# Two-layer graph and expert kernel: additions of kept outputs behind an eviction, five small loads on another queue, one part's statistics behind the first factors

## The chip, the cores and the metric

The kernel runs on one core of one Trainium2 chip. The metric is the device time of one execution in microseconds (us), lower is better. Three timed runs of the kernel before gave 2253.24, 2259.94 and 2261.37 us; the median is 2259.94. The profiled execution is another one, and its own time is in the section on the profile.

The core has TensorE (PE, with its weight loads PEld), VectorE (DVE), ScalarE (ACT), GpSimd (POOL) and SyncE (SP). Each has its own queue of instructions, which it works off in the order in which they stand there. In this kernel SP does nothing but issue DMAs; POOL and ACT issue some too.

## The reference

8192 nodes of 256 features (128 graphs of 64 nodes) pass two layers. Each layer adds a graph part and an expert part to x:

```python
# layer 0
x = x + softplus(xn @ W_self + (I - s_out*adj*s_in) @ xn @ W_neigh)   # xn: layer norm twice, gamma, beta
H = gelu(LN(x) @ W1 + b1); probs = softmax(H @ Wg + bg); e = argmax(probs)
x = x + probs[e] * (H @ Wd[e] + bd[e])                                # 8 experts, one per node
# layer 1
x = x + gelu(LN(attention(LN(x), adj)) * gamma + beta)                # attention within a graph
scores = LN(edge_softmax_sum(LN(x) @ W_gat, edge_index)).mean(heads)  # 1048576 random edges
w, top = softmax(top_k(scores, 2))                                    # 2 of 4 experts
for e in range(4):
    x = x + gate[e] * (gelu(LN(x0) @ W1[e] + b1[e]) @ W2[e] + b2[e])  # x0: x before the experts
```

All of it is float32, the matrices too.

## The kernel before

**Layout.** x stays in on-chip memory as `x[P, NT, D]`: 64 tiles of 128 nodes with 256 features. Four tiles make a group g (16 groups), two groups make a part (8 parts). The code is written as Python generators. A generator traces instructions and yields at points where another may take a turn; small loops decide whose turn it is. The trace order is then only a priority: a scheduler that has times of its own for every instruction places each on its engine's queue, and may place one ahead of others that were traced before it, if it thinks that its inputs will be there. `with tc.issue_after(ins):` adds an edge from `ins` to each instruction traced in the block on the engine of `ins`: they stand behind it on that queue. It adds no semaphore.

**The start (L418 to L577).** SP loads adjacency, x and weights in turn (L510, L142, L514). GpSimd's queue holds the making of constants, the clearing of block buffers (L522), and five small loads: b1 (L421), wg (L425), bg (L428), gcol (L526) and bcol (L528). b1, gcol and bcol are read so that feature p of a block goes to partition p: one float per element. wg is read as eight floats per element. For a part, `look` takes the statistics of its eight tiles (`bn_stats`, L548), has GpSimd copy the adjacency into block form (L553), lets TensorE sum columns into one PSUM buffer (L557), and VectorE copies the sums out (`deg`, L560). `make` works these into scale factors by about twenty small VectorE operations (L561 to L577, with L153 to L166): `fac` and `shift`. The first graph unit (`graph`, L586) has ScalarE scale x by them, and TensorE transpose the result; gcol and bcol are used as the transpose is copied out (L606). wg, b1 and bg are first used by the gated units, after about 80 us. The trace order of the start is: `look(0, -1)`, `make(-1)`, `look(1, 0)`, and then, in the mixing loop, graph units beside `make(0)` and further parts.

**The middle.** Up to 540 us graph and gating units run beside the collecting of edge keys; then the layer-0 experts of nodes sorted by expert (L928), layer 1's attention, and the edges of the second graph part. Units of the layer-1 experts (`experts`, L1068 matmuls ph, L1078 matmuls py, L1082 evictions) run beside these. In all that time the gates are not known, so outputs y are stored in DRAM (`ystore`, L1104): 28 tiles, 24 with four experts' outputs and four with three.

**The stage of pairs (about 1855 to 2164 us).** 32 of the 64 tiles are routed: their nodes are sent to slots by chosen expert, in pairs of 128-row tiles, 38 pairs in two halves. For a pair m, `pairs` loads the rows `zin` (L1990) and the expert's weights `w1e` (L1992) two pairs ahead with three buffers each, computes the hidden part in four steps (matmuls ph, L2021; gelu on ScalarE, L2025), transposes the next pair's rows (L2004), computes two output groups (matmuls py, L2034, two PSUM buffers), which VectorE evicts as `y` (L2042) and SP stores in `yslots` (L2043). It yields seven times a pair. At every third yield a step of sending or fetching rows by indirect DMA gets its turn (L1868, L2054, with the additions of L2065), and at every ninth yield a step of `kept`.

**`kept` (L1941 to L1955).** At its call n it loads the kept outputs of the nth of these 28 tiles into `yin` (L1950, two buffers, 512 or 384 KB), and adds those of tile n-1, three or four experts, each with a call of `add` (L1934): x += gate * y, 128x256. After the fourth addition of a tile its x is complete and SP stores it (L1937). The load is held behind `behind[0]`, the last w1e load or output store traced, so that it isn't issued too early on SP. The additions have no such edge. After the pairs come the units left over (from 2164 us), whose additions are made straight from y.

Of the kernel before, what the change touches and what calls it, by code (L numbers as in the profile page):

```python
# [15 lines left out]
ALU = mybir.AluOpType  # L16
# [4 lines left out]
P = 128  # L21
NT = 64
N = P * NT
D = 256
GR = 4
# [55 lines left out]
def kernel(  # L81
# [31 lines left out]
    nc = tc.nc  # L113
    V, S = nc.vector, nc.scalar
    FD = f0_w1.shape[1]
    NH = FD // P
    E0 = f0_wg.shape[1]
# [21 lines left out]
    x = const.tile([P, NT, D], F32, name="x")  # L139
# [20 lines left out]
    def moments(raw, sm, df, var):  # L160

        V.tensor_tensor(sm, raw[:, :, :, 1], raw[:, :, :, 4], ALU.add)
        V.tensor_tensor(df, raw[:, :, :, 1], raw[:, :, :, 4], ALU.subtract)
        V.tensor_tensor(var, raw[:, :, :, 2], raw[:, :, :, 5], ALU.add)
        V.scalar_tensor_tensor(df, df, 0.25, df, ALU.mult, ALU.mult)
        V.scalar_tensor_tensor(var, var, 1.0 / D, df, ALU.mult, ALU.add)  # L166
# [251 lines left out]
    with tc.tile_pool(name="w0", bufs=1, reuse_waits="tile") as w0, tc.tile_pool(name="kp", bufs=1, reuse_waits="tile") as kp:  # L418
        w1 = w0.tile([P, 2, FD], F32, name="w1")
        b1 = w0.tile([P, NH], F32, name="b1")  # L420
        nc.gpsimd.dma_start(b1, f0_b1.rearrange("(q p) -> p q", p=P))  # L421

        wg = w0.tile([P, NH, 32], F32, name="wg")
        nc.gpsimd.memset(wg, 0.0)
        nc.gpsimd.dma_start(wg[:, :, 0:E0], f0_wg.rearrange("(q p) e -> p q e", p=P))  # L425
        bg = w0.tile([P, 1], F32, name="bg")
        nc.gpsimd.memset(bg, 0.0)
        nc.gpsimd.dma_start(bg[0:E0, :], f0_bg.rearrange("(e o) -> e o", o=1))  # L428

        sel = w0.tile([P, E0], F32, name="sel")  # L430
        V.tensor_reduce(sel, ident.rearrange("p (j e) -> p e j", j=4)[:, 0:E0, :], AX.X, ALU.add)
# [16 lines left out]
        with tc.tile_pool(name="b2", bufs=2, reuse_waits="tile") as b2, tc.tile_pool(name="bh", bufs=NH + 2, reuse_waits="tile") as bh, tc.tile_pool(  # L448
# [25 lines left out]
            with tc.tile_pool(name="bg1", bufs=1, reuse_waits="tile") as bg1, tc.tile_pool(name="bg2", bufs=2, reuse_waits="tile") as bg2, tc.tile_pool(  # L474
# [48 lines left out]
                V.tensor_tensor(wcat[:, :, 0:D], wcat[:, :, 0:D], wcat[:, :, D : 2 * D], ALU.add)  # L523
                V.tensor_scalar(wcat[:, :, D : 2 * D], wcat[:, :, D : 2 * D], -1.0, None, ALU.mult)
                gcol = bg1.tile([P, 2], F32, name="gcol")
                nc.gpsimd.dma_start(gcol, g0_gamma.rearrange("(c p) -> p c", p=P))  # L526
                bcol = bg1.tile([P, 2], F32, name="bcol")
                nc.gpsimd.dma_start(bcol, g0_beta.rearrange("(c p) -> p c", p=P))  # L528

# [1 line left out]
                M = PART * GR  # L533
# [9 lines left out]
                def look(part, i):  # L543

                    raw, deg = found[i]
                    dps = psg0.tile([P, GR * P], F32, name="ms")
                    for k in range(M):
                        V.bn_stats(raw[:, 1, k, :], x[:, part * M + k, :])  # L548
                    for j in range(PART):
                        b = raws[j]  # L550
                        tsl = slice(part * M + j * GR, part * M + j * GR + GR)
                        for h in HALVES:
                            nc.gpsimd.tensor_copy(b[h, :, h], adj[h, tsl, :])  # L553
                        yield
                        for k in range(GR):
                            at = j * GR + k
                            nc.tensor.matmul(dps[:, at : at + 1], b[:, k, :], ones_col, start=True, stop=True)  # L557
                        V.tensor_reduce(deg[:, 1, j * GR : j * GR + GR], adj[:, tsl, :], AX.X, ALU.add)
                        V.tensor_scalar(on[:, tsl, :], adj[:, tsl, :], 0.0, None, ALU.is_gt)
                    V.tensor_copy(deg[:, 0, :], dps[:, 0:M])  # L560
                    yield  # L561

                def make(i):
                    raw, deg = found.pop(i)
                    sm, df, var = (bg2.tile([P, 2, M], F32, name=n) for n in ("sm", "df", "var"))
                    ve, guess, work = (bg2.tile([P, 4, M], F32, name=n) for n in ("ve", "guess", "work"))
                    moments(raw, sm, df, var)
                    V.tensor_scalar(ve[:, 0, :], var[:, 0, :], EPS, None, ALU.add)


                    V.tensor_scalar(ve[:, 1, :], var[:, 1, :], EPS, EPS, ALU.add, ALU.mult)
                    V.tensor_tensor(ve[:, 1, :], ve[:, 1, :], var[:, 1, :], ALU.add)
                    V.scalar_tensor_tensor(ve[:, 2:4, :], deg, 0.0, deg, ALU.is_equal, ALU.add)
                    to = fac[:, i + 1]
                    root_of_bits(to, ve, guess, work)
                    V.scalar_tensor_tensor(shift[:, i + 1], sm, -0.5, to[:, 0:2, :], ALU.mult, ALU.mult)
                    V.scalar_tensor_tensor(to[:, 2:4, :], deg, 0.0, to[:, 2:4, :], ALU.not_equal, ALU.mult)  # L577

                def graph(g):

# [180 lines left out]
                for _ in look(0, -1):  # L761
                    pass
                make(-1)
                next_found(0)
                for _ in look(1, 0):
                    pass
# [92 lines left out]
                last = V.tensor_copy(slot_t, es).ins  # L859

            with tc.tile_pool(name="bs", bufs=3, reuse_waits="tile") as bs, tc.tile_pool(
# [80 lines left out]
                for g in range(beside):  # L942
# [6 lines left out]
                    last = unit  # L949
# [49 lines left out]
    b1 = wp.tile([P, NEXP, NH1], F32, name="b1")  # L999
# [54 lines left out]
    to = {}  # L1054
    adds = []
    n_kept = [0] * DENSE
    pace = []
    behind = []

    def experts(g, take):  # L1060

        zT = zTs.pop(g)
        for e in range(NEXP):
            hTs = []
            for q in range(NH1):
                ph = to["ph"]()
                for c in range(2):
                    nc.tensor.matmul(  # L1068
                        ph, w1[:, e, c, q * P : q * P + P], zT[:, c, :], start=(c == 0), stop=(c == 1)
                    )  # L1070
                hT = to["hT"]()
                pace[:] = [S, S.activation(hT, ph, AF.Gelu, bias=b1[:, e, q : q + 1]).ins]  # L1072
                hTs.append(hT)
                yield "h"
            for k in range(GR):
                py = to["py"]()
                for q in range(NH1):
                    nc.tensor.matmul(  # L1078
                        py, hTs[q][:, k * P : k * P + P], w2[:, e, q, :], start=(q == 0), stop=(q == NH1 - 1)
                    )  # L1080
                y = to["y"]()
                pace[:] = [V, V.tensor_tensor(y, py, b2[:, e * D : e * D + D], ALU.add).ins]  # L1082
                take(e, k, y)
                yield "y"

# [847 lines left out]
    def add(t, e, y):  # L1933
        V.scalar_tensor_tensor(x[:, t, :], y, gate[:, e, t : t + 1], x[:, t, :], ALU.mult, ALU.add)  # L1934
        added[t] = added.get(t, 0) + 1
        if added[t] == NEXP:
            behind[:] = [nc.sync.dma_start(out_t[:, t, :], x[:, t, :]).ins]  # L1937
# [3 lines left out]
    def kept():  # L1941

        ys = {}
        ts = [t for t in range(T0) if n_kept[t // GR]]
        for n in range(len(ts) + 1):
            if n < len(ts):
                g, k = divmod(ts[n], GR)
                ys[n] = f2.tile([P, NEXP * D], F32, name="yin")[:, 0 : n_kept[g] * D]
                with tc.issue_after(behind[0]):
                    nc.sync.dma_start(ys[n], ystore[g, k, :, 0 : n_kept[g] * D])  # L1950
            if n:
                t, y = ts[n - 1], ys.pop(n - 1)
                for e in range(n_kept[t // GR]):
                    add(t, e, y[:, e * D : e * D + D])
            yield  # L1955

    with tc.tile_pool(name="gd", bufs=1, reuse_waits="tile") as gd:
# [14 lines left out]
    def pairs():  # L1972
# [39 lines left out]
        for m, (h, i) in enumerate(of):  # L2012
            e, _, w1e, b1e, b2e = loaded.pop(0)
            zT = ahead
            if m + 2 < len(of):
                loaded.append(load(*of[m + 2]))
            hTs = []
            for q in range(NH1):
                ph = to["ph"]()[:, 0 : 2 * P]
                for c in range(2):  # L2020
                    nc.tensor.matmul(  # L2021
                        ph, w1e[:, c, q * P : q * P + P], zT[:, c, :], start=(c == 0), stop=(c == 1)
                    )
                hT = to["hT"]()[:, 0 : 2 * P]
                pace[:] = [S, S.activation(hT, ph, AF.Gelu, bias=b1e[:, q : q + 1]).ins]  # L2025
                hTs.append(hT)
                yield h
            if m + 1 < len(of):
                ahead = turned(loaded[0][1])
            yield h  # L2030
            for k in range(2):
                py = to["py"]()
                for q in range(NH1):
                    nc.tensor.matmul(  # L2034
                        py,
                        hTs[q][:, k * P : k * P + P],
                        w2[:, e, q, :].rearrange("p e f -> p (e f)"),
                        start=(q == 0),
                        stop=(q == NH1 - 1),
                    )  # L2040
                y = to["y"]()
                pace[:] = [V, V.tensor_tensor(y, py, b2e, ALU.add).ins]  # L2042
                nc.sync.dma_start(yslots[h][(2 * i + k) * P : (2 * i + k + 1) * P, :], y)  # L2043
                yield h

# [99 lines left out]
```

## Time and profile before

| what | value |
|---|---|
| profiled execution, its own time | 2238.6 us |
| its span, first to last instruction | 2236.6 us |
| median of the timed runs | 2259.94 us |
| TensorE clock granted, mean | 0.966 |
| PE busy | 2072.5 us (93%) |
| DVE busy | 1526.6 us (68%) |
| ACT busy | 920.8 us (41%) |
| POOL busy | 446.6 us (20%) |

The busy time of the engines by stretch:

| stretch, us | PE busy | DVE busy | ACT busy | DMA share |
|---|---|---|---|---|
| 0 to 56 | 39.90 | 37.84 | 26.43 | 0.81 |
| 56 to 168 | 101.40 | 98.68 | 84.20 | 0.16 |
| 1855 to 1965 | 105.92 | 31.46 | 40.61 | 0.86 |
| 1965 to 2005 | 35.28 | 10.66 | 11.90 | 0.74 |
| 2060 to 2165 | 93.91 | 36.96 | 32.64 | 0.67 |
| 2165 to 2236 | 67.65 | 34.34 | 18.42 | 0.36 |

A row of the page's groups names a line, an engine, an operation and what it writes and reads, then the count, the busy time, the mean duration in ns, and how long the engine had been idle ahead of it and for whom. "SPq" is the issuing of DMAs on SyncE. A tile carved out of `wd`'s space, as most of the first stage's are, is called `wd` in the profile. A matrix product in float32 shows as two records for each matmul of the code. The difference between the profiled execution and the timed runs (21 us) is between executions of the same program.

### The profile page before, as it was taken

Reading aid. Unit: us, or ns where it says so; the run is one execution under the profiler, and the core shown is the slowest. Engines: PE = TensorE matmul, PEld = TensorE weight load, DVE = VectorE, ACT = ScalarE, POOL = GpSimd, SP = SyncE. Lnnn points to the kernel's source line nnn. Section 1 sums busy time; section 2 is a strip of 40 time slices with the busy share of each in tenths; the row PEclk is TensorE's granted clock in tenths of the full one; section 3 lists DMA queues with packets and bytes.
Section 4 is the critical chain, followed back from the end, with each engine's and each line's share of the span. In section 5 each row is a group of like instructions: output and inputs, shape, how many; then the busy total and the mean of one; then the engine's idle time right before and its main releaser. Section 6 shows DMA issues by size and latency. Waiting matters only on the chain. (4 is left out here: it accounts for less than half of the span.)

```text
span 2236.6 us, 31405 instructions
## 1 busy us (share of the span) xinstructions
PE 2072.5 (93%) x10046; PEld 1391.4 (62%) x10046; DVE 1526.6 (68%) x4539; ACT 920.8 (41%) x1662; POOL 446.6 (20%) x469
## 2 busy tenths in 40 slices
PE   7899999897999999999867889998999999999999
PEld 4444444443667667666545666765777767878776
DVE  6898997924899999994188766666788552323335
ACT  4776766664211211222157556432333333323322
POOL 3011111112000000000062100004666552303213
PEclk9999999998999999999987989999999999999999
DMA  8021122232111112112123211282222148878843
GB/s 226 25 75 50 50 65 69 79 99 76 38 55 57 38 53 57 34 53 71 46 83 119 88 40 41 77 247 58 60 58 61 43 149 251 280 223 251 257 131 98
DMA packets 206731, 219.82 MB, mean 98 GB/s; under 512 B 53200, under 2 KB 174416, under 8 KB 206560
## 3 DMA queue, kind: packets, MB, share of 16 engines
q1 hardware_dynamic: 181296, 182.37, 26.6%
q0 software_dynamic: 17056, 35.09, 5.8%
q8 instruction: 85, 1.39, 0.3%
q10 hardware_dynamic: 8208, 0.26, 0.2%
q14 instruction: 86, 0.70, 0.1%
HBM read 132.66 MB, written 84.91 MB: 97 GB/s over the span
## 5 line engine op out<-in xcount | busy, mean ns | idle before, releaser
L466 PE MATMUL ph<-zT,w 128*128 128x512 f32 x1056 | 506.6, 611 | 10.4 <-ACT zT L694 6.0
L469 ACT ACTIVATE hT<-ph,b 128x512 f32<-128x512 f32 x264 | 180.4, 686 | 492.8 <-PE ph L466 492.5
L466 PEld LDWEIGHTS ph<-zT,w 128*128 128x128 f32 x1056 | 190.5, 193 | 194.5 <-issue 169.8
L928 PE MATMUL py<-wd,hT 128*128 x1088 | 250.6, 382 | 0.0
L296 DVE TENSOR_TENSOR one<-iota_l,pb 128x1024 bf16<-128x1024 bf16 x192 | 233.2, 1215 | 1.5 <-PE cnt_ps L307 1.5
L928 PEld LDWEIGHTS py<-wd,hT 128*128 128x128 f32 x1088 | 201.0, 190 | 24.8 <-issue 0.5
L1550 POOL DMA_INDIRECT got<-tsrc,esrc x144 | 165.8, 1152 | 201.4 <-DMA zslots<-none 86.8
L1146 POOL DMA_INDIRECT yin<-yrows,row_y x64 | 64.7, 1011 | 667.3 <-SPq L991 562.5
L1078 PE MATMUL py<-w,hT 128*128 128x256 f32 x800 | 191.0, 389 | 7.3 <-DVE kt L1483 4.7
L1068 PE MATMUL ph<-zT,w 128*128 128x512 f32 x400 | 184.9, 604 | 0.0
L1078 PEld LDWEIGHTS py<-w,hT 128*128 128x128 f32 x800 | 150.3, 193 | 37.4 <-issue 13.4
L2034 PE MATMUL py<-w,hT 128*128 x608 | 142.1, 388 | 16.8 <-DVE y L2042 16.8
L1934 DVE SCALAR_TENSOR_TENSOR x<-yin,gate,x 128x256 f32<-128x256 f32 x108 | 52.1, 484 | 151.5 <-DMA yin<-ystore 149.1
L1072 ACT ACTIVATE hT<-ph,b 128x512 f32<-128x512 f32 x100 | 68.6, 687 | 210.1 <-PE ph L1068 208.5
L2025 ACT ACTIVATE hT<-ph,b1e 128x256 f32<-128x256 f32 x152 | 71.8, 473 | 199.9 <-PE ph L2021 118.6
L2021 PE MATMUL ph<-zTp,w1e 128*128 128x256 f32 x608 | 139.9, 384 | 4.1 <-DMA w1e<-in_L_ffn_W_dram 4.1
L2034 PEld LDWEIGHTS py<-w,hT 128*128 128x128 f32 x608 | 114.7, 194 | 34.2 <-DVE y L2042 19.4
L296 DVE TENSOR_TENSOR one<-iota_h,pb 128x512 bf16<-128x512 bf16 x192 | 130.7, 683 | 0.0
L2021 PEld LDWEIGHTS ph<-zTp,w1e 128*128 128x128 f32 x608 | 117.1, 193 | 20.6 <-issue 4.3
L620 PE MATMUL pre<-wd 128*128 128x512 f32 x256 | 127.8, 613 | 1.5 <-ACT wd L606 1.3
L750 POOL DMA_INDIRECT zrows<-z,pos x64 | 63.7, 995 | 281.8 <-issue 94.9
L1068 PEld LDWEIGHTS ph<-zT,w 128*128 128x128 f32 x400 | 73.6, 191 | 72.0 <-issue 71.0
(414 smaller groups left out, 3447.1 us busy)
## 6 DMA issues: line engine op xcount, KB each, us to landing
w1e<-in_L_ffn_W_dram SPq DMA_DIRECT2D x38, 512.0 KB
yin<-ystore SPq DMA_DIRECT2D x24, 512.0 KB
ystore<-y SPq DMA_DIRECT2D x80, 128.0 KB
zslots<-none SPq DMA_DIRECT2D x38, 256.0 KB
zin<-zslots SPq DMA_DIRECT2D x38, 256.0 KB
yslots<-y SPq DMA_DIRECT2D x76, 128.0 KB
zin<-zrows SPq DMA_DIRECT2D x68, 128.0 KB
bd<-in_L_ffn_bd_dram SPq DMA_DIRECT2D x68, 128.0 KB
```

Source lines behind the costliest of these rows:

```text
L296: V.tensor_tensor(o, wi.unsqueeze(1).to_broadcast([P, HK, n]), pb[:, g : g + HK].unsqueeze(2).to_broadcast([P, HK, n]), ALU.is_equal,)
L466: nc.tensor.matmul(ph, w1[:, c, q * P : q * P + P], zT[:, c, :], start=(c == 0), stop=(c == 1))
L469: gelus.append(S.activation(hT, ph, AF.Gelu, bias=b1[:, q : q + 1]).ins)
L620: nc.tensor.matmul(pre, xnT[:, c, n * P : n * P + P], wcat[:, c, :], start=(c == 0), stop=(c == 1),)
L928: nc.tensor.matmul(py, hTs[q][:, k * P : k * P + P], wd[:, bass.ds(ex[k], 1), q, :].rearrange("p e f -> p (e f)"), start=(q == 0), stop=(q ...
L1068: nc.tensor.matmul(ph, w1[:, e, c, q * P : q * P + P], zT[:, c, :], start=(c == 0), stop=(c == 1))
L1072: pace[:] = [S, S.activation(hT, ph, AF.Gelu, bias=b1[:, e, q : q + 1]).ins]
L1078: nc.tensor.matmul(py, hTs[q][:, k * P : k * P + P], w2[:, e, q, :], start=(q == 0), stop=(q == NH1 - 1))
L1550: nc.gpsimd.indirect_dma_start(got, None, tsrc, bass.IndirectOffsetOnAxis(ap=esrc[:, b, at : at + 1], axis=0))
L2021: nc.tensor.matmul(ph, w1e[:, c, q * P : q * P + P], zT[:, c, :], start=(c == 0), stop=(c == 1))
L2025: pace[:] = [S, S.activation(hT, ph, AF.Gelu, bias=b1e[:, q : q + 1]).ins]
L2034: nc.tensor.matmul(py, hTs[q][:, k * P : k * P + P], w2[:, e, q, :].rearrange("p e f -> p (e f)"), start=(q == 0), stop=(q == NH1 - 1),)
```

## The change

It does three things. `experts` and `pairs` keep the last eviction traced in `sums`, and `kept` traces its additions behind it on VectorE's queue. The five small loads at the start are issued from ScalarE's queue and not GpSimd's. `make` keeps the last instruction of each set of factors, and the second part's statistics (`look(1, 0)`) are put behind the last one of the first set; the later parts' are traced as before.

```diff
-        nc.gpsimd.dma_start(b1, f0_b1.rearrange("(q p) -> p q", p=P))
+        nc.scalar.dma_start(b1, f0_b1.rearrange("(q p) -> p q", p=P))
...
-        nc.gpsimd.dma_start(wg[:, :, 0:E0], f0_wg.rearrange("(q p) e -> p q e", p=P))
+        nc.scalar.dma_start(wg[:, :, 0:E0], f0_wg.rearrange("(q p) e -> p q e", p=P))
...
-        nc.gpsimd.dma_start(bg[0:E0, :], f0_bg.rearrange("(e o) -> e o", o=1))
+        nc.scalar.dma_start(bg[0:E0, :], f0_bg.rearrange("(e o) -> e o", o=1))
...
-                nc.gpsimd.dma_start(gcol, g0_gamma.rearrange("(c p) -> p c", p=P))
+                nc.scalar.dma_start(gcol, g0_gamma.rearrange("(c p) -> p c", p=P))
...
-                nc.gpsimd.dma_start(bcol, g0_beta.rearrange("(c p) -> p c", p=P))
+                nc.scalar.dma_start(bcol, g0_beta.rearrange("(c p) -> p c", p=P))
...
-                    for k in range(M):
-                        V.bn_stats(raw[:, 1, k, :], x[:, part * M + k, :])
+                    with tc.issue_after(first_made[0]) if part == 1 else ExitStack():
+                        for k in range(M):
+                            V.bn_stats(raw[:, 1, k, :], x[:, part * M + k, :])
...
-                    V.scalar_tensor_tensor(to[:, 2:4, :], deg, 0.0, to[:, 2:4, :], ALU.not_equal, ALU.mult)
+                    last = V.scalar_tensor_tensor(to[:, 2:4, :], deg, 0.0, to[:, 2:4, :], ALU.not_equal, ALU.mult)
+                    first_made.append(last.ins)
+
+                first_made = []
...
                 pace[:] = [V, V.tensor_tensor(y, py, b2[:, e * D : e * D + D], ALU.add).ins]
+                sums[:] = pace[1:]
...
-                for e in range(n_kept[t // GR]):
-                    add(t, e, y[:, e * D : e * D + D])
+                with tc.issue_after(sums[0]):
+                    for e in range(n_kept[t // GR]):
+                        add(t, e, y[:, e * D : e * D + D])
...
                 pace[:] = [V, V.tensor_tensor(y, py, b2e, ALU.add).ins]
+                sums[:] = pace[1:]
```

More of the change, by code (lines that the diff above doesn't have):

```diff
@@ L1057 @@
     pace = []
+    sums = []
     behind = []
```

## The prediction, made before the changed kernel was run

> **What bounds the kernel now.** I read four views, in this order: the chain of waits on the page, the waits of the stage 1850 to 2165 us, that stage's busy time in windows with the timelines of three engines around one stall, and the timelines of the first 35 us. The chain reaches back only to 1519 us, where a loop guard joins all engines; before that the busy table must do, and there TensorE is busy 93% of the span.
>
> ```profile
> PE 26%; DMA 3%; DVE 1%; issue 1%; SPq 1%; POOL 0%; ACT 0%; DVEq 0%; ACTq 0%; POOLq 0%
> PE py L1078 7%; PE ph L1068 6%; PE py L2034 5%; PE ph L2021 4%; DMA yin<-ystore 2%; PE pd L1562 1%; PE ps L1594 1%; PE ph L2004 0%; DMA w1e<-in_L_ffn_W_dram 0%; PE ps L1500 0%; DVE x L1934 0%; DVE y L2042 0%; DMA yslots<-y 0%; DVE x L2065 0%; DMA zslots<-y,place 0%
> ```
>
> The reader is to see that the end is set by matmuls, and that the one large entry beside them is a load: yin<-ystore, the kept expert outputs that `kept` fetches (L1950). 2% of 2236.6 us is 45 us of chain. Not all of it is lost: matmuls run during part of it. The waits of the stage say who passes it on:
>
> ```profile
> DVE x L1934 <- DMA yin<-ystore: 149.1, 25, 10.3
> ...
> DVE y L2042 <- PE py L2034: 49.3, 24, 12.3
> ...
> PEld py L2034 <- DVE y L2042: 19.4, 11, 4.4
> PE py L2034 <- DVE y L2042: 16.8, 8, 4.2
> ```
>
> Columns: us waited in total, times, longest. VectorE waits 149 us in 25 waits at L1934, the additions; that alone costs nothing. But TensorE then waits for VectorE's evictions (L2042), because the additions stand ahead of these on VectorE's queue. One stall in full (VectorE, SyncE and TensorE lines of their timelines):
>
> ```profile
> 1991.15 0.75 DVE L2042 TENSOR_TENSOR y<-py,b2e 128x256 f32<-128x256 f32 x2
> 2002.25 1.01 DVE L1934 SCALAR_TENSOR_TENSOR x<-yin,gate,x 128x256 f32<-128x256 f32 x2 [10.35 <-DMA yin<-ystore]
> 2003.17 0.42 DVE L2042 TENSOR_TENSOR y<-py,b2e 128x256 f32<-128x256 f32 x1
> ...
> 1995.47 0.42 SPq L1950 DMA_DIRECT2D yin<-ystore  x1
> ...
> 2003.64 5.41 PE L2034 MATMUL py<-w,hT 128*128 x16 [4.12 <-DVE y L2042]
> ```
>
> The load is issued at 1995.47 and lands at 2002.2; the eviction behind it follows at 2003.17, and TensorE, with both py buffers full, starts 4.12 us late. Its group takes 5.41 us where undisturbed ones take 3.46 (the second half waits again): 1.95 us more, 6.1 us in all.
>
> How much is lost in all? By the chain, py groups of successive pairs start at 1866.17 and, thirteen pairs on, at 1961.89: 7.36 us a pair. From 1961.89 to the stage's end at 2163.79 are 201.9 us; 24 pairs at 7.36 and one last py group of 3.46 are 180.1. So **21.8 us** are lost, all after 1962 (the first thirteen pairs hide VectorE's waits of up to 8.4 us).
>
> At the start:
>
> ```profile
> 7.42 0.78 POOL L526 DMA_DIRECT2D gcol<-in_L_gnn_gamma_dram  x1
> 9.14 1.75 POOL L553 COPY wd<-wd 64x256 f32<-64x256 f32 x4
> ...
> 10.82 1.73 DVE L548 BATCH_NORM_STATS2 raw<-x 128x6 f32<-128x256 f32 x5 [1.02 <-DMA x<-in_x_dram]
> 13.00 0.69 DVE L523 TENSOR_TENSOR wd<-wd 128x512 f32<-128x512 f32 x1 [0.45 <-DMA wd<-in_L_gnn_W_neigh_dram]
> 16.29 0.75 DVE L548 BATCH_NORM_STATS2 raw<-x 128x6 f32<-128x256 f32 x2
> 20.84 0.17 DVE L560 COPY deg<-ms 128x8 f32<-128x8 f32 x1 [1.21 <-PE ms L557]
> 23.04 0.16 DVE L576 SCALAR_TENSOR_TENSOR shift<-sm,fac 128x16 f32<-128x16 f32 x1
> ...
> 23.24 2.57 ACT L586 ACTIVATE wd<-x,shift,fac 128x256 f32<-128x256 f32 x5 [11.09 <-DVE shift L576]
> ```
>
> ScalarE begins the first graph unit at 23.24 us, on factors finished at 23.1. The first part's statistics and moments are through at 16.29; then the second part's eight statistics are threaded into the chain of small factor operations, and at 20.84 it also waits for the second part's degree copy.
>
> **What the skill says.** (1) The Trainium skill, "DMA: Bandwidth & Descriptors", section "Anatomy of one DMA", says that DMA engines don't wait on semaphores: the wait is on the issuing sequencer. The trace agrees: SyncE issued one pair's w1e at 1961.64 straight after an output store at 1961.05, whose additions ended at 1961.0. A late addition thus holds other loads too. (2) The same page, "Rules for kernel authors", says that a strided last dimension becomes one descriptor per element; no view read here counts descriptors for the small loads, but a like load on SyncE (b1, L1009, 2048 single floats) occupied its issue for 2.47 us. (3) The same page, "Issuing engines are not separate DMA queues": moving a load to another issuer saves that issuer's time only. The trace's DMA share of 0.83 to 1.15 in the first 40 us shows the engines they all share to be full then.
>
> **The change part by part.**
>
> *Additions behind an eviction.* `kept` is called at every ninth yield of `pairs`, which yields seven times a pair. Tile t's additions are therefore traced at yield 9t+17, behind 2 x floor((9t+17)/7) evictions, plus 1 or 2 where the remainder is 5 or 6. The new edge makes that the earliest place. Counting L2042 ahead of each L1934 group on VectorE gives today's place: tile 10 has 28 evictions ahead and gets at least 30; tile 13, 34 and 38; tile 16, 44 and 46; tile 19, 51 and 54; tile 23, 62 and 64; tile 24, 64 and 66; tile 25, 67 and 68. Over tiles 0 to 26 the gain is 0 to 4 evictions, mostly 2 to 4, each 7.36 / 2 = 3.7 us of matmul. The longest wait is 10.35 us, at tile 13, which gains 14.7 us; tile 10's 9.71 us meets 7.4 us, but only the part past its own eviction's readiness was lost (0.6 us there). No instruction is added. Behind the waiting addition stand the next evictions and output stores; the load of tile t+2 takes tile t's buffer (two buffers), so it must not be pushed late. By trace order, load t+2 follows w1e of two pairs ahead, which is free when the previous pair's hidden matmuls end. The latest case has its additions behind the second eviction of two pairs before that; they need 0.4 + 4 x 0.5 = 2.4 us of the 3.45 us of those hidden matmuls, so they finish about 1 us ahead. From load issue to the additions at least py, hidden and py again lie: 10.8 us against 6.7 us measured above. Tile 25 gains one eviction only and tile 18 none; I leave 3 us of the 21.8. Bounds: 22 gained if no load is late, 8 if half the waits come back through SyncE's queue. I take **19**.
>
> *Second part's statistics behind the first factors.* Eight at 0.34 us apart (1.73 us for five) leave the chain: 2.7 us. The 1.21 us wait can go as well: with no fillers the chain may end before the second part's degree copy, which stays free to move. So 2.7 to 3.9, upper value taken. They run right after; their user is the second factors, whose scaling starts at 32.09 on ScalarE, 9 us later, so that is the cover.
>
> *Small loads to ScalarE's queue.* GpSimd loses 1.09 + 0.93 + 0.56 + 0.78 + 0.74 = 4.1 us of issuing; its copies (9.14) can start near 5.6, where the adjacency has landed. That is hidden: the statistics wait for x until 10.82. ScalarE gains five issues; at 0.5 to 2.5 us each (SyncE's usual issue and the L1009 one) that is 2.5 to 12.5 us from about 1 us on, and it does nothing else until 23.24. By one element per descriptor they make 1024 + 1024 + 8 + 512 = 2568 packets. On ScalarE's queue now, 8208 packets take 0.2% of 16 engines' span, 8.7 ns each; 2568 x 8.7 / 16 = 1.4 us that x and W_neigh may land later. An estimate: bounds 0 and 4 us, should issues of SyncE queue up behind them; I take 1.4. gcol and bcol are needed at 26.3 today, near 22 then.
>
> Start: 3.9 - 1.4 = **2.5 us**, bounds -2 and 5. From there TensorE is busy 90% or more, so a head start is kept; other work is threaded anew in the first 540 us, which can give or take 3 us.
>
> Sum: 19 + 2.5 = 21.5. Against the profiled execution (2238.6 us, span 2236.6) that is 2217; the timed runs lie 21 us above it, and the loss is of the same nature there, so I take it off their median: 2259.94 - 21.5 = **2238**.
>
> **Rivals.**
> - *The transfer takes the place of the queue.* Evictions flow, but yin, w1e and outputs are issued late on SyncE and pairs wait for weights. For it: the DMA share of 0.86 in 1855 to 1965, and one SyncE queue for all. Against: those thirteen pairs ran at full rate at that share. Gain 8 at the least, 0 at the start: 2252.
> - *Slower: the load's buffer.* If additions end up later than traced by over about 1 us past the hidden matmuls, SyncE stops at each yin load with the next w1e behind it. w1e is issued two pairs ahead, 14.7 us, of which landing takes 6 to 7 and SyncE's lag about 3; below 5 us of stop it is free, beyond that each of 26 loads pays the excess. At 6.5 us of stop: 26 x 1.5 = 39 lost on top of a gain of 19: 2280. For it: two buffers only, 1 us of margin. Against: the scheduler places additions where their eviction is due, and a full pair more is needed.
> - *The start goes the other way.* Small packets delay x and W_neigh by 4 us, factors come 2 us later or are rethreaded badly: 2260 - 19 + 5 = 2246.
> - *The edge moves nothing* would be 2260; the counts above exclude it for tiles 10 to 25.
>
> **How the numbers follow.** Forecast 0.62, start the other way 0.14, transfer 0.14 (with the last rival), slower 0.10. What this measurement can tell from no change is 0.5%, 11.3 us: faster 0.76, same 0.14, slower 0.10. Forecast alone: gains of 12 to 27, 2233 to 2248. The timed runs scatter from 2253 to 2261, and the transfer rival at 2252 is taken in: 2226 to 2254.
>
> **What would show it.** Right: L1934's waits for yin fall from 149 us to a few, TensorE's waits for L2042 vanish, py groups keep 7.36 us through 2164; L576 near 19 to 21 us, and L586 follows it. Wrong: TensorE waiting for w1e or zin; yin issued later against its pair than today; the first L548 after 12 us; a first graph unit held by gcol or bcol at L606.

## The result, and the profile after

| | before | after |
|---|---|---|
| median of 5 timed runs, us | 2259.94 (2251.79 to 2262.57) | 2237.92 (2232.50 to 2241.17) |
| profiled execution, us | 2238.6 | 2232.5 |
| its span, us | 2236.6 | 2230.4 |

The ratio is 0.9909, 95% interval 0.9881 to 0.9936: 22 us less, between 14 and 27. The two profiled spans differ by 6.2 us only, so the profiles have to be read stretch by stretch before the 22 us are found in them. I take marks that both have: the first `shift`, the last scatter of the layer-0 gating, the last store of the layer-0 experts, the first gather of the edges, the first and the last py matmul of the pairs. "Attention" is from the last expert store to the first gather, "edges" from there to the first py.

```
                     first   gating  experts  edges   first   last    atten-
                     shift   end     end      begin   py      py      tion    edges   pairs   span
before                23.0   549.0   1109.0   1506.3  1866.0  2163.4  397.3   359.7   297.4   2236.6
after                 21.6   545.4   1105.4   1509.3  1882.6  2157.2  403.9   373.3   274.6   2230.4
```

The pairs lost 22.8 us. 3.6 us came up to the end of the gating, and 20.2 us were given back in attention and edges, in which nothing was changed: from the first attention step to the first pairs, every engine has the same instructions in the same order in both kernels. Those 20.2 us are what the first and the last experiment are about.

The pairs first. The chain of waits of the changed kernel, as the page has it:

```profile
PE 29%; DVE 2%; issue 1%; DMA 0%; another core or an unknown queue 0%; SPq 0%; DVEq 0%
PE py L1084 6%; PE ph L1074 6%; PE ph L2030 6%; PE py L2043 6%; PE ps L1601 2%; PE pd L1569 2%; PE ph L2013 1%; DVE rows L1500 0%; PE ps L1507 0%; DMA w1e<-in_L_ffn_W_dram 0%; DVE y L1088 0%; DVE ol L1457 0%; PE ps L1531 0%; DVE to L1563 0%
```

Lines have moved: the additions are now L1941, the pairs' matmuls ph and py L2030 and L2043, their evictions L2051, the load of yin L1957. The load of the kept outputs, 2% before, is gone from the chain, and the shares of both kinds of pair matmuls are larger. The waits from 1840 to 2160 us (us in total, times, longest):

```profile
DVE y L2051 <- PE py L2043: 139.5, 60, 12.2
...
DVE x L1941 <- DMA yin<-ystore: 5.9, 5, 2.6
...
PE ph L2030 <- DMA w1e<-in_L_ffn_W_dram: 3.9, 1, 3.9
```

VectorE's 149 us of waiting for yin have become 5.9, and it waits for TensorE in their place, 139.5 us, as one expects where TensorE is the bound. In this view TensorE doesn't wait for an eviction any more; its one wait is for the first pair's weights. VectorE's timeline at one such place:

```profile
1987.40 0.42 DVE L2051 TENSOR_TENSOR y<-py,b2e 128x256 f32<-128x256 f32 x1 [3.24 <-PE py L2043]
1989.13 0.42 DVE L2051 TENSOR_TENSOR y<-py,b2e 128x256 f32<-128x256 f32 x1 [1.30 <-PE py L2043]
1989.78 2.05 DVE L1941 SCALAR_TENSOR_TENSOR x<-yin,gate,x 128x256 f32<-128x256 f32 x4 [0.23 <-DMA yin<-ystore]
1994.75 0.42 DVE L2051 TENSOR_TENSOR y<-py,b2e 128x256 f32<-128x256 f32 x1 [2.92 <-DMA out_dram<-x]
```

Two evictions, then four additions, then about 3 us of nothing until the next pair's outputs are due. (The view puts the last wait down to a store; the py group whose first half that eviction takes had begun at 1992.98.) Before, the additions stood ahead of two evictions and held them. The stage's timeline on the chain gives a pair every 7.35 us without a break, from 1882.79, where the first pair's py group starts, to 2157.6.

The start, with VectorE's lines and then GpSimd's, TensorE's and ScalarE's from their own timelines:

```profile
10.04 1.74 DVE L550 BATCH_NORM_STATS2 raw<-x 128x6 f32<-128x256 f32 x5 [1.26 <-DMA x<-in_x_dram]
13.75 0.15 DVE L562 COPY deg<-ms 128x8 f32<-128x8 f32 x1
17.62 0.17 DVE L562 COPY deg<-ms 128x8 f32<-128x8 f32 x1 [3.21 <-PE ms L559]
21.60 0.17 DVE L578 SCALAR_TENSOR_TENSOR shift<-sm,fac 128x16 f32<-128x16 f32 x1
21.78 2.70 DVE L550 BATCH_NORM_STATS2 raw<-x 128x6 f32<-128x256 f32 x8
24.42 0.40 DVE L600 TENSOR_TENSOR wd<-wd,fac 64x256 f32<-64x256 f32 x1
33.54 0.17 DVE L578 SCALAR_TENSOR_TENSOR shift<-sm,fac 128x16 f32<-128x16 f32 x1
...
6.51 1.89 POOL L555 COPY wd<-wd 64x256 f32<-64x256 f32 x4 [2.02 <-DMA wd<-in_adj_dram]
...
25.40 1.09 PE L617 MATMUL tz<-ident,wd 128*128 128x128 f32 x4 [0.77 <-DVE wd L600]
...
1.35 0.89 ACTq L425 DMA_DIRECT2D wg<-in_L_ffn_Wg_dram  x1
2.27 1.46 ACTq L526 DMA_DIRECT2D gcol<-in_L_gnn_gamma_dram  x1
```

Before, the scaling and the second factors stood here:

```profile
23.65 0.40 DVE L595 TENSOR_TENSOR wd<-wd,fac 64x256 f32<-64x256 f32 x1
29.80 0.17 DVE L576 SCALAR_TENSOR_TENSOR shift<-sm,fac 128x16 f32<-128x16 f32 x1
```

GpSimd's copies do start sooner (6.51 for 9.14), and x isn't later for the small loads (10.04 for 10.82). The statistics of the second part are out of the chain: they run in one piece after the factors. But the second part's degree copy has stayed in it and costs 3.21 us in place of 1.21. The first factors come 1.4 us sooner (over all profiles with the same start 21.2 to 21.6 us, where three of the start before have 22.3 to 23.0). What follows them is not all sooner: the first unit's adjacency scaling (L600), at 23.65 before, is now behind the eight statistics at 24.42, and TensorE waits 0.77 us for it; and the second factors come at 33.54, where they came at 29.80.

### The profile page after: what moved, and what is told of

Same layout as the page of the kernel before. It is cut to its first block, busy times and chain, and to the rows that moved or that the text cites. A ratio compares the mean times of both kernels' runs of the same rounds, so it can differ in the third digit from the quotient of the medians.

```text
span 2230.4 us, 31413 instructions
## 1 busy us (share of the span) xinstructions
PE 2067.0 (93%) x10046; PEld 1387.5 (62%) x10046; DVE 1526.1 (68%) x4539; ACT 922.5 (41%) x1663; POOL 441.3 (20%) x464
## 5 line engine op out<-in xcount | busy, mean ns | idle before, releaser
L2030 PE MATMUL ph<-zTp,w1e 128*128 128x256 f32 x608 | 140.0, 384 | 3.9 <-DMA w1e<-in_L_ffn_W_dram 3.9
L2051 DVE TENSOR_TENSOR y<-py,b2e 128x256 f32<-128x256 f32 x76 | 32.2, 424 | 157.3 <-PE py L2043 139.5
L2043 PE MATMUL py<-w,hT 128*128 x608 | 137.5, 379 | 0.0
L2030 PEld LDWEIGHTS ph<-zTp,w1e 128*128 128x128 f32 x608 | 117.2, 193 | 20.5 <-issue 4.1
L2043 PEld LDWEIGHTS py<-w,hT 128*128 128x128 f32 x608 | 112.6, 190 | 13.8
```

The source lines that it names most:

```text
L2030: nc.tensor.matmul(ph, w1e[:, c, q * P : q * P + P], zT[:, c, :], start=(c == 0), stop=(c == 1))
L2043: nc.tensor.matmul(py, hTs[q][:, k * P : k * P + P], w2[:, e, q, :].rearrange("p e f -> p (e f)"), start=(q == 0), stop=(q == NH1 - 1),)
```

## The experiments

Ratios are to the kernel before on the same chip. The first four rows are from one chip, the next four from a second and the last two from a third; the chips of the first two profiles, above, are not on record. The rows without a ratio were run once. This table has the same marks for all of them:

```
                              first   gating  atten-
                              shift   end     tion    edges   pairs   span     ratio, 95% interval
before, second profile         22.3   546.8   407.2   367.5   296.9   2251.4   -
additions' edge only           22.3   544.7   407.4   372.8   274.6   2233.2   0.9902 [0.9876, 0.9927]
start only                     21.5   544.5   414.1   370.0   297.0   2258.7   1.0006 [0.9991, 1.0021]
degree copy behind factors     17.6   543.3   414.2   376.8   274.6   2241.8   0.9900 [0.9874, 0.9925]
loads only                     23.4   550.7   407.2   374.0   290.8   2255.6   -
statistics only                22.0   546.8   410.4   366.6   297.3   2254.3   -
edge two evictions back        21.2   542.6   404.0   373.2   290.6   2243.4   0.9961 [0.9946, 0.9977]
additions a call later         21.6   547.1   413.7   369.5   275.2   2238.2   0.9923 [0.9897, 0.9949]
scaling first                  17.4   542.3   397.3   359.6   274.6   2207.0   0.9901 [0.9882, 0.9920]
after, second profile          21.4   543.2   397.2   359.3   274.6   2207.4   0.9905 [0.9887, 0.9924]
```

**The kernel before again**, with no edit.

> The kernel before, unchanged, for a second profile. In the two profiles shown, the stretch from the edges' first gathers to the first pair's py group (1506.3 to 1866.0 us before, 1509.3 to 1882.6 after) differs by 13.6 us, though VectorE, TensorE and ScalarE have the same instruction order there. If that is run-to-run (my theory), this profile's stretch lies elsewhere between 355 and 380 us and need not be 360. If the change made that stretch longer (rival), it is 358 to 362 again. In the pairs, 20 to 24 us of stall again under both.

Attention and edges took 9.9 and 7.8 us longer than in the first profile of the same program. That is 17.7 us between two profiles of one program, where the kernel before and the changed one differed by 20.2. The edges alone, at 367.5 us, are neither the first profile's 359.7 nor the changed kernel's 373.3. The pairs differ by 0.5 us.

**One half at a time.** The kernel before with the additions' edge alone:

```diff
+                sums[:] = pace[1:]
...
+                with tc.issue_after(sums[0]):
```

> Only the additions' edge, the start as before. My theory: the 38 pairs take 38 x 7.35 us without stall, VectorE's waits at the additions for yin fall below 10 us; timed 18 to 22 us under before (ratio 0.990 to 0.992). Rival (the gain in the timed runs comes from the start): ratio above 0.996.

And the changed kernel without that edge:

```diff
-                with tc.issue_after(sums[0]):
+                if True:
```

> The loads on ScalarE's queue and the statistics' edge, no edge on the additions. My theory: first factors near 21.6 us as in after, 1.4 us sooner, growing to about 3.6 us by 549 us; the pairs stall 20 to 24 us as before; timed 2 to 4 us under before (ratio 0.998 to 0.999). Rival: 15 us or more of the gain is here, ratio below 0.994.

The additions alone give the whole: 274.6 us of pairs and 0.9902. The start alone gives nothing that can be measured, 1.0006; its interval leaves at most 2 us. Its first factors are as early as in after, but the mark at the end of the gating says nothing: 544.5 with the start's changes and 544.7 without them. The 3.6 us that I read off the first pair of profiles at that mark can't be told from scatter: three profiles of the start before have 544.7 to 549.0 there, five of the changed start 542.6 to 547.1. The 2 to 4 us that I expected of the start in the timed runs didn't show. The stalls of the pairs are all there in the start-only kernel (waits from 1850 to 2190 us):

```profile
DVE x L1941 <- DMA yin<-ystore: 122.6, 24, 11.1
...
PE py L2043 <- DVE y L2051: 12.5, 4, 4.1
```

**A dose of the edge.** `sums` keeps three evictions, and the additions stand behind the oldest:

```diff
-                sums[:] = pace[1:]
+                sums[:] = [*sums, *pace[1:]][-3:]
```

> The changed kernel with the additions behind the eviction two before the last one, so that they stand two evictions further ahead than in after (tile 10 behind 28, as before; tile 13 behind 36, between 34 and 38). My theory, that the place on VectorE's queue is the whole of it: between before and after, VectorE waits 30 to 90 us for yin and the pairs take 280 to 290 us (274.6 in after, 297 before). Rival (any edge will do): 275 to 277.

The waits of that stage:

```profile
DVE x L1941 <- DMA yin<-ystore: 88.7, 17, 8.7
...
PEld py L2043 <- DVE y L2051: 9.2, 6, 4.2
PE py L2043 <- DVE y L2051: 7.7, 4, 4.0
```

88.7 us stand between 149 and 5.9, and 290.6 us of pairs between 297 and 274.6, just past the upper end of what was expected. By the pairs alone this dose couldn't be told from no edge, since the loads-only kernel further down, with the places of before, has 290.8. The timed runs tell them apart: 0.9961, at most 0.9977, where the start alone is at least 0.9991.

The waits tell more, tile by tile. Nine of the tiles that waited before (1, 2, 5, 6, 8, 9, 12, 13 and 15) have one or two more evictions ahead of their additions in this kernel than before. Their waits for yin were 52.6 us together before and are 0.3 us here. Tile 19 gains one eviction for its first addition only and waits as before (4.8 for 4.2). The others that waited, among them those of the late stalls (20 and 22 to 26), have as many evictions ahead as before, and still wait 83.5 us (92.4 before). An edge as such isn't enough: the additions' place on the queue is what counts.

**The price of lateness.** The rival on the slower side said that additions placed too late hold the load that takes their buffer, and the weights behind it. Here each tile's additions come one call of `kept` later, directly ahead of the load that needs their buffer:

```diff
-        for n in range(len(ts) + 1):
+        for n in range(len(ts) + 2):
+            if n > 1:
+                t, y = ts[n - 2], ys.pop(n - 2)
+                with tc.issue_after(sums[0]):
+                    for e in range(n_kept[t // GR]):
+                        add(t, e, y[:, e * D : e * D + D])
             if n < len(ts):
...
-            if n:
-                t, y = ts[n - 1], ys.pop(n - 1)
...
```

> The changed kernel with each tile's additions one call of kept later, ahead of the load that takes their buffer: still two buffers, so SyncE reaches each load of yin while its buffer's additions are still to come. The slower rival of the prediction says that this holds w1e back behind it: with a stop of 6.5 us at each of 26 loads the pairs take 300 us or more. My theory: the stop is at most about 6 us after w1e is issued, inside the two pairs by which w1e runs ahead, and the pairs take 275 to 279 us, the whole within 5 us of after.

The pairs took 275.2 us. No addition waited for yin at all, and TensorE's only wait for weights in that stage was the first pair's:

```profile
PE ph L2030 <- DMA w1e<-in_L_ffn_W_dram: 4.0, 1, 4.0
```

So the additions may come two to four evictions later than in the changed kernel at no cost that shows; two evictions earlier cost 16 us of the pairs in the profiles, 13 in the timed runs (0.9961 for 0.9902). But the stop that the rival speaks of hardly arose. SyncE's longest listed wait for an addition, at the store of x ahead of the load, was 1.4 us (8 waits, 7.9 us in all), since VectorE ran the additions straight behind their eviction. What a stop of 6.5 us would cost was not tried.

**The start's two parts alone.**

The first is the kernel before with `nc.scalar` for `nc.gpsimd` in all five loads:

```diff
-        nc.gpsimd.dma_start(b1, f0_b1.rearrange("(q p) -> p q", p=P))
+        nc.scalar.dma_start(b1, f0_b1.rearrange("(q p) -> p q", p=P))
...
```

> The kernel before with the five small loads on ScalarE's queue and nothing else. My theory: GpSimd's first adjacency copies start near 6.5 us in place of 9.1, the first statistics at 10 to 10.8 us (no harm from the small packets), and the first shift stays at 22 to 23 us, as the second part's statistics and degree copy still stand in its chain. Rival (the loads make the gain at the start): first shift at 21.6 us, as in after.

The second is the kernel before with the statistics' edge:

```diff
+                    with tc.issue_after(first_made[0]) if part == 1 else ExitStack():
```

> The kernel before with the second part's statistics behind the first factors and nothing else. My theory: the eight statistics leave the chain, but VectorE then stands at the second part's degree copy, which waits for TensorE's sums, and the first shift comes at 21.5 to 24 us: with the copies on GpSimd starting at 9.1 us the sums come later than in after. The first graph unit's adjacency scaling is behind the statistics, some 2.7 us after the factors in place of 0.6. Rival (the edge alone brings the start forward): first shift under 21 us and the scaling within 1 us of it.

Neither part brings the factors forward by much by itself: 23.4 us (a little over the expected 22 to 23) and 22.0, where the two profiles of the kernel before have 23.0 and 22.3. Both kernels stand at the second part's degree copy, on VectorE, the loads-only one first:

```profile
17.48 0.17 DVE L560 COPY deg<-ms 128x8 f32<-128x8 f32 x1 [3.21 <-PE ms L557]
```

and with the statistics only:

```profile
19.74 0.17 DVE L562 COPY deg<-ms 128x8 f32<-128x8 f32 x1 [2.86 <-PE ms L559]
22.05 0.40 DVE L578 SCALAR_TENSOR_TENSOR shift<-sm,fac 128x16 f32<-128x16 f32 x1
22.45 2.70 DVE L550 BATCH_NORM_STATS2 raw<-x 128x6 f32<-128x256 f32 x8
25.09 0.40 DVE L600 TENSOR_TENSOR wd<-wd,fac 64x256 f32<-64x256 f32 x1
```

The scaling, 0.6 us after the first shift before the change, is 3.0 us after it here. (The loads-only kernel's pairs took 290.8 us with the additions at the same places as before. Four other profiles without the edge have 296.9 to 297.4, so what the stalls come to varies by some 6 us; the cause of that was not looked for.)

**The degree copy too.** The copy that stood in the chain is put behind the first factors:

```diff
-                    V.tensor_copy(deg[:, 0, :], dps[:, 0:M])
+                    with tc.issue_after(first_made[0]) if part == 1 else ExitStack():
+                        V.tensor_copy(deg[:, 0, :], dps[:, 0:M])
```

> The changed kernel, with the second part's degree copy also behind the first factors on VectorE's queue. In after VectorE stood 3.21 us at that copy ahead of the chain of factors. My theory: first shift at about 18.4 us in place of 21.6, and 2 to 3 us off the whole (about 2235). Rival: the second factors become late for the third graph unit, and nothing is gained: 2238, with ScalarE waiting at the scaling of x at 30 to 36 us for longer than the 0.6 us of after.

The first shift came at 17.6 us, 4.0 sooner than in after. The first unit's logarithm, its last activation, came at 40.48 for 41.95, so at most 1.5 of the 4 us were left 23 us on. It may be less: the same start has the logarithm anywhere from 40.4 to 42.0 us in five profiles. The 2 to 3 us that were expected off the whole didn't show either: the timed ratio, 0.9900, can't be told from that of the additions alone on the same chip, 0.9902.

**The scaling first.** To see what had eaten the rest, the statistics were also traced after the first unit's scaling:

```diff
...
                     def factors():
                         yield
+                        if i == 0:
+                            with tc.issue_after(first_made[0]):
+                                stats(1, found[0][0])
                         make(i)
...
```

> The changed kernel with the second part's degree copy behind the first factors, and its statistics traced after the first graph unit's adjacency scaling, so that on VectorE the factors are followed by the copy, the scaling and only then the statistics. My theory: first shift near 17.6 us as with the degree copy alone, scaling within 1 us of it, the first graph unit's last activation (the logarithm) 1 to 2 us ahead of the 40.5 us seen there; by 545 us at most 3 us of it left, and the whole within 4 us of after, under before by 20 us or more. Rival (a head start is kept in full): 5 us or more under after.

VectorE did as meant (shift, copy, scaling, statistics):

```profile
17.42 0.26 DVE L582 SCALAR_TENSOR_TENSOR shift<-sm,fac 128x16 f32<-128x16 f32 x1
17.69 0.15 DVE L566 COPY deg<-ms 128x8 f32<-128x8 f32 x1
17.82 0.55 DVE L604 TENSOR_TENSOR wd<-wd,fac 64x256 f32<-64x256 f32 x1
18.39 0.53 DVE L604 TENSOR_TENSOR wd<-wd,fac 64x256 f32<-64x256 f32 x1
18.94 2.71 DVE L545 BATCH_NORM_STATS2 raw<-x 128x6 f32<-128x256 f32 x8
```

Yet the logarithm came at 40.05 us, 0.4 ahead of the kernel with the degree copy alone, not 1 to 2, and 0.9 ahead of the changed kernel on the same chip (40.94). The wait is now on TensorE and then ScalarE:

```profile
18.16 3.58 PE L562 MATMUL ms<-ones_col,wd 128*128 128x1 f32 x16 [0.75 <-POOL wd L558]
21.59 1.95 PE L614 MATMUL tz<-ident,wd 128*128 128x128 f32 x8
...
23.36 1.45 ACT L615 ACTIVATE wd<-tz,bcol,gcol 128x512 f32<-128x512 f32 x2 [3.09 <-PE tz L614]
```

The column sums of a third part, 3.58 us of one-column matmuls, stand on TensorE ahead of the first unit's transposes. In the kernel with the degree copy alone they stood just behind the first of these transposes, and ahead of those of the adjacency:

```profile
18.72 2.16 PE L611 MATMUL tz<-ident,wd 128*128 128x128 f32 x8 [1.53 <-ACT wd L592]
20.95 3.54 PE L559 MATMUL ms<-ones_col,wd 128*128 128x1 f32 x16
24.35 1.09 PE L618 MATMUL tz<-ident,wd 128*128 128x128 f32 x4
```

So the adjacency's transposes came at 24.35 and, with the scaling first, at 24.20, where the changed kernel has them at 25.40: of the 4 us about 1 was left there already. In both versions the unit that was released sooner ran into work of a later part on another engine's queue. At the end of the gating the mark is 542.3 for 543.2, inside the scatter, and the medians are 2209.67 and 2210.33 us: no version was found that is faster than the changed kernel by more than can be measured.

**The changed kernel again**, beside it on the same chip.

> The changed kernel unchanged, beside the one with the scaling first on the same chip. My theory: the pairs take 274 to 275 us again; the stretch of attention and the one of edges, in which nothing was changed, differ from the first profile's by up to 15 us together, as they do between two profiles of the kernel before; timed at 0.988 to 0.993 of before. Rival (the long edge stretch of 373 us belongs to the change): 372 to 375 us again.

The pairs took 274.6 us again, and attention and edges 397.2 and 359.3, as in the very first profile of the kernel before; against the first profile of the changed kernel they are 20.7 us shorter together, more than the 15 expected. So the changed program can have both stretches as short as the kernel before had them, and the 20.2 us that the first two profiles gave back don't belong to the change.

## Why the prediction was right, step by step

**The total**: 2238 forecast, 2237.92 measured, with 0.62 on this case. That agreement is luck: the additions gave about 3 us more than forecast and the start about 2.5 less, and the measured gain itself is only known to lie between 14 and 27 us.

**Where the loss is and why**: right. 21.8 us were said to be lost after 1962 us. With the edge alone the pairs took 22.3 to 22.8 us less, and with the edge two evictions back just those tiles stopped waiting whose additions had moved.

**What the edge recovers**: mis-sized. I left 3 us for tiles that gain one eviction or none (25 and 18), so 19; nothing was left, the term is 22 to 23 us, at the upper bound of 22 and just past it. The places on VectorE's queue came out as worked out from the trace order (28 to 30 for tile 10, 34 to 38 for tile 13, 67 to 68 for tile 25), and the remaining 5.9 us of waiting hold no eviction for which TensorE waits. The tiles for which I left the 3 us waited less as well: tile 18 2.6 us for 7.1 at an unchanged place, tile 25 1.8 for 8.6. That earlier stalls had made their loads late before is the likely reason; it was not tested.

**The statistics out of the chain**: the step that failed. The first shift, announced for 19 to 21 us, came at 21.6. "The 1.21 us wait can go as well: with no fillers the chain may end before the second part's degree copy" did not happen: the copy stayed in the chain, and with nothing else to do there VectorE stood 3.21 us. "They run right after; their user is the second factors" overlooked another user of the queue: the first unit's adjacency scaling stood behind them, and the second factors were late as well (33.54 for 29.80). I had counted the wait that goes, and not what stands behind the moved instructions on their own queue.

**The small loads**: right in kind. GpSimd's relief was hidden (its copies began at 6.51, held by the adjacency's load, and not near 5.6). No harm came: the first statistics began at 9.6 to 10.1 us in the eight profiles with the loads on ScalarE's queue and at 10.1 to 10.8 in the four others, where I had charged 1.4 us. What I had named as the worse case, issues of SyncE queueing up, did occur: its second load of x was issued at 6.4 to 6.7 us in place of 4.4 to 4.8, but no engine is seen to wait for that load; the five issues took 3.9 us on ScalarE in the first profile of the changed kernel (0.48, 0.89, 1.46, 0.50 and 0.53), below the middle of the bounds.

**The start as a whole**: 2.5 us forecast, 1.4 at the first factors, none that shows in the timed runs (1.0006, at most 2 us). "A head start is kept" failed too: 4.0 us at the first factors, with the degree copy behind them or the scaling first, had become about 1 at the adjacency's transposes and 0.9 to 1.5 at the end of the first unit, no more than profiles with the same start differ by there.

**The rivals**: "transfer takes the place" is refuted, w1e delayed TensorE once, as before. "Slower: the load's buffer" didn't occur, and a full call's delay of the additions wasn't enough to bring it about (SyncE's longest wait 1.4 us); how long a stop the loads could bear stays open. "The start goes the other way" didn't occur.

**The timed runs above the profile**: that the loss "is of the same nature there" was a guess, and it held: the pairs took 296.9 us in the second profile of the kernel before, whose execution took 2253.59 us. Most of the 21 us by which the first profile lay below the timed runs is found in two stretches that the change doesn't touch: they were 17.7 us shorter in it than in the second.

## What to carry to other kernels

VectorE's waits for a load cost nothing in the first thirteen pairs of the kernel before; they cost where they stood ahead of the eviction that frees the bound engine's buffer for longer than that engine had work. So look for the pair "A waits for DMA" and "bound engine waits for A", and put what waits behind the eviction that is due: here the last two evictions of the move (7 us of matmuls) were worth 13 to 16 us of the 22, and a further move did no harm. At the start, a chain freed of one thing gave little, because the next engine had other work at the head of its queue; follow the head start unit by unit before counting it. When two profiles are compared, split them into stretches first, and don't credit the change with a difference in a stretch in which the order of instructions is the same in both until a second profile of the same kernel has been taken.

## What the runs showed of the hardware that was not expected

The same program, the kernel before, takes 2233 us (median of 9) on one chip and 2255 to 2257 us (medians of 19 and 24) on two others. By the profiles of the changed kernel and its variants, of which each chip has some, most of the difference lies in two stretches, attention (397.2 to 397.3 us there, 404.0 to 414.2 on the others) and edges (359.3 to 359.6, and 366.6 to 376.8). On one chip, too, they differ between profiles, by up to 10 us each. The layer-0 experts (560 us from the end of the gating) and the pairs with the additions in their new places or later (274.6 to 275.2) agree within 1 us on all. Both stretches hold indirect gathers by GpSimd, but no single wait in the traces carries the difference, and its cause stays open. The first profile of the kernel before (397.3 and 359.7) looks like the fast chip, the first of the changed kernel (403.9 and 373.3) like the others.

The five small loads are few packets from one issuer and many from the other. The page's DMA queues of the changed kernel (packets, MB, share of 16 engines):

```profile
q0 software_dynamic: 16896, 35.05, 5.7%
q10 hardware_dynamic: 10848, 0.30, 0.3%
```

GpSimd's queue had 17056 packets before and ScalarE's 8208: 160 packets went and 2640 came. I had counted 2568, one for each element or run of eight floats, which comes near on ScalarE's queue only. The views count packets and not descriptors, so how many elements a packet of GpSimd's queue carries isn't shown.
